# A selective-scan, attention and feed-forward kernel on one core: 32 channels by 4 states on the partitions, scans that end in PSUM, and a new set of due times

## The chip, the cores and the metric

One core of a Trainium2 chip runs the whole program in one launch. The metric is the device time of the launch in microseconds (us); smaller is better. Five engines work side by side: TensorE (PE) multiplies matrices into PSUM, VectorE (DVE) and ScalarE (ACT) work on SBUF and PSUM, GpSimd (POOL) works on SBUF, and SyncE (SP) issues the transfers here.

## The reference, cut to what matters

The input `x` has 8 images of 384 channels by 32x32 positions, 1024 tokens each. Per image the reference does this (all float32):

```
xn   = rmsnorm over channels of x
mamba(xn) forward, and backward over the reversed tokens:
    u, z  = split(in_proj(xn));   u = silu(causal conv over 4 tokens of u)
    dt, Bm, Cm = split(x_proj(u));  delta = softplus(dt_proj(dt))
    h[c, n, t] = exp(delta[c, t] * A[c, n]) * h[c, n, t-1] + delta[c, t] * u[c, t] * Bm[n, t]
    y[c, t]    = sum over 16 states n of h[c, n, t] * Cm[n, t]  + u * D
    result     = out_proj(y * silu(z))
y1   = x + res_scale * (scale_mod * (fwd + bwd) + sigmoid(3x3 depthwise conv of xn) * xn)
y2   = y1 + causal attention(layernorm(y1)) with rotary q and k
out  = feed-forward with gelu of layernorm(y2), plus y2
```

The recurrence over `t` for each of 384 channels and 16 states, in two directions, is the bulk of the elementwise work: 384 x 16 x 1024 x 2 values per image.

## The kernel before, in words

**Order.** Nothing in this kernel is issued where it is written. The class `Plan` records each instruction with a due time, measured in "units" of the scan (`plan.due`), and a `rush`; then `Plan.order` goes through a list schedule with its own cost for each kind of instruction, hands out the buffers named by `plan.tile(pool, shape, tag, bufs)`, and writes one fixed order for each engine. So all recorded instructions have the same line in the profile (the call in `issue`), and they are told apart by their tiles. Every engine works through its own list strictly in that order, and the lists depend on the constants at the head of the file: `SCAN`, `OTHERS`, `LAYER1` and so on are due times, and the numbers in `Plan` are costs. `_fill` adds matmuls of zeros (`y<-zero,ident`) where the planner sees TensorE idle; they add nothing to the sum in `y` and only keep TensorE busy.

**The scan.** An image has four steps (two directions by two halves of 512 tokens, `HB = 512`). A step is cut into 12 units (`n_u = NU * SG`). In a unit, the 128 partitions hold `CG` = 16 channels by `NE` = 8 states, and the free dimension holds `NQ` = 4 further channels of 512 tokens each, 2048 elements in all. A group of 64 channels takes `SG` = 2 units, one for each half of the 16 states. The tiles of a unit:

- `dl` (delta) and `du` (delta times u) are loaded from HBM (`dd`, `db`), each channel's row repeated on its 8 partitions: four transfers of 128x512 for each, once per group. `du` lies in a buffer of the tag `hs`, of which there are 5; `dl` has 5 buffers of 512.
- `br` and `cr` hold B and C, repeated over the channels: two loads of each per step. ACT copies `cr` into two PSUM banks, `cb`.
- POOL forms `hs = du * br` over 2048 elements.
- ACT forms `da = exp(dl * A)` four times, 512 elements each, in PSUM; the tag `da` has 3 banks.
- DVE runs `tensor_tensor_scan` four times, from `da` and `hs` into `hs`.
- In the steps where a half is followed by the next one, ACT copies the last column of `hs` to `carry`.
- `hs = hs * C` over 2048 elements, on DVE with `cb`, or on POOL with `cr` for the units in `POOL_C` (4 of 12) or `POOL_END`.
- PE sums over the states: four matmuls with the 0/1 matrix `sel` add the four quarters of `hs` to 32 rows each of the one PSUM bank `y`. Only then is the `hs` buffer free.

After the last unit of a 128-channel block, `y` leaves PSUM, either through ACT to `yd` in HBM or through DVE, times silu(z), to `side`.

**The rest**, spread between the units by `plan.spread`: `norm_in` (rmsnorm and the first half of in_proj; `xn` holds both halves of an image), `conv_tokens`, `prepare` (x_proj, dt_proj, softplus; writes `dd`, `db`, `bd`), `local_branch` (`gate`: the other half of in_proj; `conv`: the 3x3; `local`), then `project`, `attention` and `feed_forward` of the tokens that are done. Matmuls of these take one of two PSUM banks `w`; eight banks in all: 2 `w`, 3 `da`, 2 `cb`, 1 `y`. ACT has to load another table for silu, gelu or softplus and then again for exp.

Of the kernel before, what the change touches and what calls it, by code (L numbers as in the profile page):

```python
# [27 lines left out]
ALU = mybir.AluOpType  # L28
# [9 lines left out]
RUSH = 3.54  # L38
# [4 lines left out]
FIRST = (1.62, 3.88, 10.08, 14.37, 18.13, 22.35)  # L43
SECOND = (23.0, 0.55)
OTHERS = (4.41, 9.05, 14.9, 16.09, 22.99, 26.51, 31.92, 33.87, 42.68, 49.8)
BURST = 8.0
PROJECT = 1.86
LAYER1 = (39.24, 51.32, 61.95, 72.21, 83.3)
LAYER1_6 = (40.54, 50, 58.1, 65.96, 73.04)
LAYER1_7 = (39.38, 43.03, 45.9, 58.42, 62.69, 67.55, 71.01, 75.01, 81.01)  # L50
HASTE = 22.72
FREE = ["w", "da", "cb", "w", "da", "cb", "da"]
EXPS = 0.0
SCAN = (-1.59, -1.1, -0.46, -0.4, -0.36, 0.15, 0.79, 1.19)
class _Op:
# [4 lines left out]
        "busy", "early", "succ", "left", "ready", "preds", "issued",  # L60
# [16 lines left out]
class Plan:  # L77
# [8 lines left out]
    SWITCH = 1.3  # L86
    LOOSE = ("w", "tmp", "side")
    HURRY = 7.31
    PATIENCE = 1.81
    SETTLE = 0.2  # L90
    HOP = 0.18
    RATE = 300e3
    LAND = 2.54
    GATE = 3.413
    WARM, COLD = 0.8, 0.45
    KEEP = 0.65
    AHEAD = 9.0
# [41 lines left out]
    def add(self, eng, call, method, args, kw):  # L139
# [8 lines left out]
        op.tail, op.bytes = self.HOP, 0  # L148
        op.table, op.batch = None, self.batch
        if method == "dma_start":  # L150
            op.bytes = math.prod(outs[0].shape) * 4
            op.cost = 0.45 if eng == "sync" else 1.0
        elif eng == "tensor":
            once = kw.get("is_transpose") or method == "transpose"

            m = outs[0].shape[0]
            rate = 1.05 if once else 0.62 if m <= 32 else 1.0 if m <= 64 else 1.72
            op.cost = 0.02 + rate * max(n, 96) / 1e3
            op.busy = 0.75 if once else min(1.0, ins[0].shape[0] / 96)
            op.tail += self.SETTLE  # L160
        elif eng == "vector":
            scan = method == "tensor_tensor_scan"
            op.cost = 0.14 + (2.09 if scan else 1.04) * n / 1e3
            if method == "scalar_tensor_tensor":
                op.cost += 0.06
            if method in ("tensor_copy", "bn_aggr"):
                op.cost = 0.16
        elif eng == "scalar":
            aps = sum(1 for k, v in kw.items() if k in ("scale", "bias") and isinstance(v, bass.AP))
            op.cost = 0.21 + 0.714 * n / 1e3 + 0.05 * (method == "activation") + 0.06 * aps + 0.2 * ("accum_out" in kw)  # L170
            op.table = self.SETS.get(args[2]) if method == "activation" else self.set
        elif eng == "gpsimd":
            op.cost = (0.45 + 1.0 * n / 1e3) if len(ins) == 1 else (0.1 + 2.165 * n / 1e3)
# [93 lines left out]
    def _fill(self, t, now, begun):  # L267
# [5 lines left out]
        while work < self.KEEP * self.GATE:  # L273
# [3 lines left out]
            op.cost, op.busy, op.bytes, op.table = 0.02 + 1.72 * n / 1e3, 1.0, 0, None  # L277
# [8 lines left out]
    def order(self):  # L286
# [14 lines left out]
        drained = 0.0  # L301
# [53 lines left out]
        while issued < total:  # L355
# [36 lines left out]
            if op.bytes:  # L392
                drained = max(drained, end + 0.3) + op.bytes / self.RATE
                done = drained + self.LAND
                clock[e] = max(end, drained - self.AHEAD)
# [11 lines left out]
            for o in op.succ:  # L407
                o.left -= 1
                o.ready = max(o.ready, end if o.eng == e and not op.bytes else done)
# [17 lines left out]
def conv_attn_kernel(  # L427
# [31 lines left out]
    CG = 16  # L459
    NE = P // CG  # L460
    SG = NS // NE
    NQ = 4
    NU = C // (NQ * CG)
# [14 lines left out]
    def bank():  # L478
        rota.append(rota.pop(0))
        if rota[-1] == "w":  # L480
            return plan.tile(ps_w, [P, HB], "w", 2)
        return plan.tile(ps_b, [P, HB], rota[-1])
# [36 lines left out]
    dtw = weight([P, 2, C], "dtw")  # L519
    plan.vector.memset(dtw, 0.0)  # L520
    for d in range(2):
        plan.sync.dma_start(dtw[d * HP : d * HP + R, d], dt_wT)
# [42 lines left out]
    for to, at, n in ((up, 0, UP), (up, L + UP, UP), (xq, 0, WP + 1), (xq, XP - WP, WP)):  # L565
# [8 lines left out]
        logs.rearrange("c (j s) -> c j s", s=NQ * NS),  # L574
        a_log.rearrange("(j c q) n -> c j (q n)", c=CG, q=NQ),
# [25 lines left out]
    turn = "p (r q) -> p q r"  # L601
    for cc in range(NC):
        plan.gpsimd.tensor_scalar(
            ddiag[:, cc].rearrange("p (q r) -> p q r", q=NQ), ident.rearrange(turn, q=NQ),
            v_d[:, cc : cc + 1], None, ALU.mult,
        )

    held = weight([P, CG], "held")
    plan.vector.reduce_sum(held, ident.rearrange("p (c n) -> p c n", n=NE), axis=AX.X)
    sel = weight([P, 2, 2 * CG], "sel")  # L610
    plan.vector.memset(sel, 0.0)
    for i in range(2):
        plan.vector.tensor_copy(sel[:, i, i * CG : (i + 1) * CG], held)
# [34 lines left out]

    raw = plan.tile(l0, [P, NQ, HB], "hs", 5).rearrange("p q t -> p (q t)")[:, : NC * C]
    raw = raw.rearrange("p (cc e) -> p cc e", cc=NC)  # L650
    plan.sync.dma_start(raw, in_wT[:, C:].rearrange("(cc p) e -> p cc e", p=P))
    wz = weight([P, NC, C], "wz")
    for cc in range(NC):
        for m in range(NC):
            cols = slice(m * P, (m + 1) * P)
            plan.gpsimd.tensor_copy(
                wz[:, cc, cols].rearrange("p (q r) -> p q r", q=NQ),
                raw[:, cc, cols].rearrange(turn, q=NQ),
            )
    wout = weight([P, NC, C], "wout")  # L660
    for cc in range(NC):
        plan.sync.dma_start(
            wout[:, cc], out_wT[cc * P : (cc + 1) * P].rearrange("(r q) e -> q r e", q=NQ)
        )
# [47 lines left out]
    xn_t, z_t = {}, {}  # L712
# [11 lines left out]
    def xn_of(b, h):  # L724

        return xn_t[b][:, :, h * HR : (h + 1) * HR, :W]

    def norm_in(b, h):
        xt = load_x(b, h)
        yield  # L730
        if b not in xn_t:
            xn_t[b] = plan.tile(l0, [P, NC, H, WP], "xn")
        xn = xn_of(b, h)
# [13 lines left out]
        padded = xn_t[b][:, :, h * HR : (h + 1) * HR]  # L747
# [8 lines left out]
        for m in range(NC):  # L756
# [10 lines left out]
            yield  # L767

# [31 lines left out]
    def local(b, h):  # L800
# [6 lines left out]
        for cc in range(NC):  # L807
            xt = tmp()
            plan.sync.dma_start(xt, xv[b, :, cc, cols])
            sgi = sg[:, cc].rearrange("p (r w) -> p r w", w=W)  # L810
            plan.gpsimd.tensor_mul(sgi, sgi, xn_of(b, h)[:, cc])
# [4 lines left out]
    def gate(b, h):  # L816

        z = z_t[b, h] = plan.tile(l0, [P, NC, HB], "uc", 2)
        for m in range(NC):
            pz = bank()  # L820
            for cc in range(NC):
                plan.tensor.matmul(
                    pz.rearrange("p (r w) -> p r w", w=W),
                    wz[:, cc, m * P : (m + 1) * P], xn_of(b, h)[:, cc],
                    start=cc == 0, stop=cc == NC - 1,
                )
            plan.scalar.copy(z[:, m], pz)
            yield
# [47 lines left out]
    def prepare(b, steps):  # L876
# [17 lines left out]
        for i, si in enumerate(steps):  # L894
# [3 lines left out]
                [plan.tile(dram, [NC * 2 * CG, NQ * HB], nm, 8) for nm in ("dd", "db")]  # L898
# [4 lines left out]
        def rates(i, cc):  # L903
            pd = bank()
            rows = len(steps) * HP
            plan.tensor.matmul(
                pd, dtw[:rows, i, cc * P : (cc + 1) * P], xd[:rows], start=True, stop=True
# [3 lines left out]
        def store(i, cc, pd):  # L911
# [6 lines left out]
            for kd, t in zip(kept[i], (dl, du)):  # L918

                rows = kd[cc * 2 * CG : (cc + 1) * 2 * CG]  # L920
                plan.sync.dma_start(rows.rearrange("r (q t) -> (r q) t", q=NQ), t)
# [26 lines left out]
    def scan(b, si, lo=0, hi=HB):  # L948
# [9 lines left out]
        br = []  # L958
        for g in range(SG):
            plan.due = t0 + g - 4.0  # L960
            br.append(plan.tile(l0, [P, HB], "br", 2)[:, :n])
# [3 lines left out]
        plan.due = t0 - 1.5  # L965
        cr = plan.tile(l0, [P, SG, HB], "cr")[:, :, :n]
        cb = []
        for g in range(SG):
            plan.due = t0 - 1.5 + 0.2 * g
            plan.sync.dma_start(  # L970
                cr[:, g], bd[NS + g :: SG, lo:hi].unsqueeze(0).to_broadcast([CG, NE, n])
            )
            plan.due = t0 + f * (g - 0.3)
            cb.append(plan.tile(ps_b, [P, HB], "cb", SG)[:, :n])
            plan.scalar.copy(cb[g], cr[:, g])

# [3 lines left out]
        def hold():  # L980
            if not pair:
                t = plan.tile(l0, [P, NQ * HB], "hs", 5)
                for o in range(0, NQ * HB, NQ * n)[:SG] if n < HB else (0,):
# [3 lines left out]
        for k in range(n_u):  # L987
            q, g = divmod(k, SG)
            cc, part = divmod(q, 2)
            t = t0 + f * k  # L990
            if g == 0:
                rows = slice(q * CG, (q + 1) * CG)
                plan.due = t - 3.6
                du = hold()

                begin = b == 0 and si == 0 and k == 0
                for i in range(NQ):
                    plan.sync.dma_start(
                        du[:, i],
                        db[rows, i * HB + lo : i * HB + hi].unsqueeze(1).to_broadcast([CG, NE, n]),  # L1000
                    )
                plan.due = t - 3.4
                dl = []
                for i in range(NQ):
                    if i * n % HB == 0:
                        both = plan.tile(l0, [P, HB], "dl", 5)
                    dl.append(both[:, i * n % HB : i * n % HB + n])
                    plan.sync.dma_start(
                        dl[-1],
                        dd[rows, i * HB + lo : i * HB + hi].unsqueeze(1).to_broadcast([CG, NE, n]),  # L1010
                    )
                if part == 0:
                    plan.due = t - 2.0
                    parts = []
                    if ud is not None:
                        parts.append((ddiag[:, cc], ud[cc * P : (cc + 1) * P, lo:hi]))
                    if si >= 2:
                        parts.append((ident, y_t[b, h, cc][:, lo:hi]))
# [455 lines left out]
```

## Time and profile before

| what | value |
|---|---|
| time, three runs | 3198.13 us median (3196.02 to 3198.74) |
| the profiled execution: span | 3199.6 us, granted TensorE clock 0.964 |
| PE busy | 2770.0 us (87%), of which the matmuls of zeros 349.7 us |
| POOL busy | 2693.5 us (84%) |
| DVE busy | 2675.7 us (84%) |
| ACT busy | 2189.8 us (68%), 160 table loads of 1283 ns among it |
| DMA | 762.47 MB, 78.5% of 16 engines' span on SP's queue |

The span is that of the profiled execution, which is the one whose durations are used below; it lies 1.5 us over the median, within a thousandth. "Busy" is the time with at least one instruction of the engine running; a busy PE can still be waiting in part, since matmuls are pipelined and their ends modelled. In the lists of waits, a row "A x <- B y: us, times, longest" says how long engine A stood idle ahead of an instruction that writes tile x until engine B's instruction that writes y ended. "L423" stands in all of them.

### The profile page before, as it was taken

The page shows a single profiled execution, that of the slowest core. Times are in us where ns is not written, and L with a number is a line of the kernel's source. Part 1 is how long each engine was busy: PE and PEld are TensorE (multiplying, and loading weights), DVE is VectorE, ACT ScalarE, POOL GpSimd, SP SyncE. Part 2 cuts the span into 40 slices and gives each one's busy share as a digit, 9 for nine tenths or more (in the row PEclk, how much of TensorE's full clock was granted, in tenths as well). Part 3 has the DMA queues.
Part 4 walks back from the last instruction along what each step waited for, and adds up shares of the span by engine and source line. Part 5 has one row for each costly group of instructions (what it writes and reads, how often), then busy time and mean ns, then how long its engine had stood idle before and what let it go on. Part 6 is the DMA issues. An engine that isn't in the chain of part 4 may idle for free. (4 is left out here: it accounts for less than half of the span.)

```text
span 3199.6 us, 39939 instructions
## 1 busy us (share of the span) xinstructions
PE 2770.0 (87%) x11855; PEld 1160.9 (36%) x11855; DVE 2675.7 (84%) x2740; ACT 2189.8 (68%) x3591; POOL 2693.5 (84%) x923
## 2 busy tenths in 40 slices
PE   7887888888988989899888888898898998787789
PEld 3323333343333334343333433334343433343345
DVE  3778778897898889997899978988799979998972
ACT  3566676867677776868578676767768686666564
POOL 2888887788998889889889888888898989998950
PEclk9998999999999999999999998999999999999899
DMA  7998997878979887887978788798878879665530
GB/s 232 289 293 259 285 286 224 260 230 260 265 229 279 250 248 242 270 251 239 266 239 268 237 252 249 223 279 243 262 236 258 259 237 279 196 197 175 174 100 12
DMA packets 424462, 762.47 MB, mean 238 GB/s; under 512 B 51020, under 2 KB 70804, under 8 KB 424244
## 3 DMA queue, kind: packets, MB, share of 16 engines
q1 hardware_dynamic: 424116, 759.80, 78.5%
q8 instruction: 93, 1.52, 0.2%
q14 instruction: 125, 1.02, 0.1%
q0 software_dynamic: 128, 0.11, 0.0%
HBM read 617.92 MB, written 141.80 MB: 237 GB/s over the span
## 5 line engine op out<-in xcount | busy, mean ns | idle before, releaser
L423 POOL TENSOR_TENSOR hs<-hs,br 128x2048 f32<-128x2048 f32 (+1 forms) x395 | 1737.6, 4406 | 312.6 <-PE y L423 156.1
L423 ACT ACTIVATE da<-dl,nega 128x512 f32<-128x512 f32 (+1 forms) x1584 | 1056.6, 677 | 534.5 <-DVE hs L423 384.0
L423 DVE TENSOR_TENSOR_SCAN hs<-da,carry,hs 128x512 f32<-128x512 f32 (+1 forms) x816 | 935.7, 1201 | 125.1 <-ACT da L423 113.7
L423 DVE TENSOR_TENSOR_SCAN hs<-da,hs 128x512 f32<-128x512 f32 x768 | 883.9, 1202 | 132.6 <-ACT da L423 115.5
L423 POOL TENSOR_TENSOR hs<-hs,cr 128x2048 f32<-128x2048 f32 (+1 forms) x137 | 599.0, 4372 | 30.1 <-DVE hs L423 23.3
L423 DVE TENSOR_TENSOR hs<-hs,cb 128x2048 f32<-128x2048 f32 (+1 forms) x259 | 574.1, 2217 | 44.4 <-ACT carry L423 38.4
L423 PE MATMUL y<-hs,sel 128*32 128x512 f32 (+1 forms) x3168 | 446.7, 607 | 91.2 <-POOL hs L423 54.5
L423 PE MATMUL y<-zero,ident 128*128 128x256 f32 x1304 | 349.7, 398 | 0.0
L423 PEld LDWEIGHTS y<-zero,ident 128*128 128x128 f32 x1304 | 237.9, 195 | 144.7 <-issue 121.4
L423 PE MATMUL w<-rep,cit 96*32 96x512 f32 x1152 | 199.2, 657 | 34.1 <-DMA rep<-xq 26.3
L421 ACT ACT_TABLE_LOAD x160 | 205.3, 1283 | 2.8
L423 PE MATMUL w<-v,p 128*128 128x384 f32 x546 | 196.5, 506 | 10.4 <-ACT p L423 9.3
L423 PEld LDWEIGHTS y<-hs,sel 128*32 128x32 f32 x3168 | 80.9, 110 | 339.3 <-DVE hs L423 128.6
L423 PE MATMUL w<-q,fc1s 128*128 128x512 f32 (+1 forms) x388 | 191.0, 607 | 12.8 <-ACT p L423 6.0
L423 PE MATMUL w<-rep,cwt 128*32 128x512 f32 x744 | 162.1, 613 | 28.8 <-DMA rep<-up 13.6
L423 PE MATMUL w<-wout,side 128*128 128x384 f32 x378 | 146.4, 515 | 31.7 <-DVE side L423 22.3
L423 ACT ACTIVATE uc<-w,vec 128x512 f32<-128x512 f32 x144 | 97.1, 680 | 109.4 <-PE w L423 91.4
L423 ACT COPY gl<-w 128x512 f32<-128x512 f32 (+2 forms) x254 | 136.7, 549 | 23.4 <-PE w L423 21.2
L423 PE MATMUL w<-xn,wz 128*128 128x512 f32 x288 | 135.5, 614 | 11.3 <-ACT uc L423 5.0
L423 PEld LDWEIGHTS w<-v,p 128*128 128x128 f32 x546 | 101.4, 194 | 100.3 <-ACT p L423 31.2
L423 PE MATMUL w<-xn,win 128*128 128x512 f32 x288 | 133.5, 605 | 4.6 <-ACT tmp L423 4.4
L423 PE MATMUL w<-wvs,gl 128*128 128x384 f32 x372 | 135.4, 502 | 0.8 <-ACT uc L423 0.6
(204 smaller groups left out, 3191.8 us busy)
## 6 DMA issues: line engine op xcount, KB each, us to landing
dl<-dd SPq DMA_DIRECT2D x744, 256.0 KB, 5.4
hs<-db SPq DMA_DIRECT2D x744, 256.0 KB, 5.6
rep<-up SPq DMA_DIRECT2D x180, 257.5 KB, 6.4
rep<-xq SPq DMA_DIRECT2D x192, 222.4 KB, 7.1
tmp<-in_x_dram SPq DMA_DIRECT2D x96, 256.0 KB, 5.4
dd<-tmp SPq DMA_DIRECT2D x96, 256.0 KB, 3.7
db<-uc SPq DMA_DIRECT2D x96, 256.0 KB, 4.2
br<-bd SPq DMA_DIRECT2D x62, 256.0 KB, 5.8
```

The source lines that it names most:

```text
L421: self.nc.scalar.preload_act_table_set(table)
L423: op.call(*args, **{k: self._bind(v) for k, v in op.kw.items()})
```

## The change

Four things change together.

1. **Layout.** `CG` = 32 channels by `NE` = 4 states lie on the partitions, so `SG` = 4 units share one group of 128 channels, and there are three groups in a step, not six. `dl` and `du` are loaded three times per step; `br` and `cr` are four loads each. `sel` has one form; `wz`, `wout` and `ddiag` need no permuted columns. The number of units, exponentials and scans stays.
2. **Scan in PSUM.** In units whose multiply by C is on DVE (`split`), each scan writes over its exponential `da`, the carry is copied from there, one column for each scan, and DVE multiplies `hs[:, i] = da * cr[g]` 512 elements at a time. `cb` is gone, and `da` has 5 banks. The four matmuls of such a unit have due times of their own. Units with the multiply on POOL stay as they were.
3. **Input by halves.** `xn` holds one half. The gate's matmuls run right after `norm_in` (`raw_gate`), their result goes to HBM (`zr`) and comes back in `gate`; `local` loads `xn` from `xq`.
4. **Costs and due times** of the planner are other numbers: matmuls, ScalarE, transfers (with eight lanes for SP), and all constants of the schedule.

```diff
-SCAN = (-1.59, -1.1, -0.46, -0.4, -0.36, 0.15, 0.79, 1.19)
+SCAN = (-1.68, -1.03, -0.46, -0.42, -0.39, 0.15, 0.05, 1.19, 0.92)
+DU_AHEAD = 3.6
+DL_AHEAD = 4.52
+DLS = 5
+DAS = 5
...
-            rate = 1.05 if once else 0.62 if m <= 32 else 1.0 if m <= 64 else 1.72
-            op.cost = 0.02 + rate * max(n, 96) / 1e3
+            rate = 0.85 if once else 0.43 if m <= 32 else 0.84 if m <= 64 else 1.676
+            op.cost = rate * max(n, 64) / 1e3
...
-    CG = 16
+    CG = 32
...
-    NQ = 4
-    NU = C // (NQ * CG)
+    NQ = P // CG
+    NU = NC
...
+    def raw_gate(b, h):
+
+        xn, z = xn_t[b, h], plan.tile(dram, [P, NC, HB], "zr", 4)
+        zr_t[b, h] = z
+        for m in range(NC):
+            pz = bank()
+            for cc in range(NC):
+                plan.tensor.matmul(
+                    pz.rearrange("p (r w) -> p r w", w=W),
+                    wz[:, cc, m * P : (m + 1) * P], xn[:, cc],
+                    start=cc == 0, stop=cc == NC - 1,
+                )
+            zt = tmp()
+            plan.scalar.copy(zt, pz)
+            plan.sync.dma_start(z[:, m], zt)
+            yield
...
+            xn = reps()[:, : HR * WP]
+            at = 1 + (h * HR + 1) * WP
+            plan.sync.dma_start(xn, xq[cc * P : (cc + 1) * P, at : at + HR * WP])
...
-            cb.append(plan.tile(ps_b, [P, HB], "cb", SG)[:, :n])
-            plan.scalar.copy(cb[g], cr[:, g])
...
+            split = k not in (POOL_END if b == NB - 1 else POOL_C)
...
-                da = plan.tile(ps_b, [P, HB], "da", 3)[:, :n]
+                da = plan.tile(ps_b, [P, HB], "da", DAS)[:, :n]
...
-                o, a = hs[:, i], da
+                o, a, r = hs[:, i], da, da if split else hs[:, i]
...
-                plan.vector.tensor_tensor_scan(o, a, o, init, ALU.mult, ALU.add)
...
+                plan.vector.tensor_tensor_scan(r, a, o, init, ALU.mult, ALU.add)
+                if split:
+                    if save:
+                        plan.due, plan.rush = t + f * SCAN[5] * (i + 0.1), RUSH
+                        plan.scalar.copy(carry[:, k, i : i + 1], da[:, 0:1] if d else da[:, n - 1 :])
+                        plan.rush = 0.0
+                    plan.due = t + f * (SCAN[5] * i + SCAN[6])
+                    plan.vector.tensor_mul(hs[:, i], da, cr[g])
...
-                plan.vector.tensor_mul(hs, hs, cb[g].unsqueeze(1).to_broadcast([P, NQ, n]))
...
             for i in range(NQ):
+                plan.due, plan.rush = t + f * (SCAN[7] - 0.2 * (NQ - 1 - i) * split), RUSH
                 plan.tensor.matmul(
-                    y[i * 2 * CG : (i + 1) * 2 * CG], sel[:, part], hs[:, i],
-                    start=False, stop=done, skip_group_check=True,
+                    y[i * CG : (i + 1) * CG], sel, hs[:, i],
+                    start=g == 0 and not parts, stop=done, skip_group_check=True,
```

The program as built differs in these counts (before, after): matmuls of zeros 652, 916; DVE multiplies by C 259 (245 of 2048 elements, 14 of 1024), 1036 (980 of 512, 56 of 256); scans 1584, 1584, of which 1036 now write `da`; ACT copies to `carry` 204, 603; ACT copies to `cb` 66, none; table loads 161, 157; POOL's multiplies unchanged, its nine copies to `wz` gone; SP's transfers 2998, 2448.

## The prediction

> **What bounds it now.** I read the engines' shares first, then windows, then the waits of the engines that carry the scan, then a stretch of timeline that shows one of those waits.
>
> ```profile
> PE 2770.0 (87%) x11855; PEld 1160.9 (36%) x11855; DVE 2675.7 (84%) x2740; ACT 2189.8 (68%) x3591; POOL 2693.5 (84%) x923
> ...
> 800.00:2800.00 2000.00, 1759.90 (x7622) 723.08 (x7626) 1781.36 (x1767) 1436.78 (x2328) 1793.85 (x594) 0.97 0.83 250
> ```
>
> In the 2000 us in the middle (second row; columns PE, PEld, DVE, ACT, POOL busy), DVE is at 89% and POOL at 90%. No engine is full; two are nearly so and each waits for the other. The first 160 us (POOL busy 88) and the last 100 (POOL 10) are start and tail, and little in them changes. What can be won is the idle time in between. Waits of DVE, POOL and ACT (us, times, longest):
>
> ```profile
> DVE hs L423 <- ACT da L423: 229.2, 91, 6.8
> DVE hs L423 <- ACT carry L423: 38.6, 22, 5.2
> ...
> POOL hs L423 <- PE y L423: 156.1, 49, 10.5
> POOL hs L423 <- DMA hs<-db: 70.8, 15, 31.4
> ...
> ACT da L423 <- DVE hs L423: 384.0, 485, 5.2
> ACT da L423 <- DMA dl<-dd: 117.7, 87, 5.0
> ```
>
> DVE is idle 3199.6 - 2675.7 = 524 us; its largest wait is for exponentials. POOL is idle 506 us; its largest wait is for PE to free an `hs` buffer. Yet ACT itself waits 384 us for a free `da` bank: it could run ahead and has nowhere to write. The timeline of ACT and DVE shows how that hurts:
>
> ```profile
> 1498.43 1.28 ACT L421 ACT_TABLE_LOAD   x1
> 1499.72 2.77 ACT L423 ACTIVATE gl<-gl 128x3072 f32<-128x3072 f32 x1
> 1502.39 0.57 ACT L423 COPY uc<-w 128x512 f32<-128x512 f32 x1
> 1502.98 1.28 ACT L421 ACT_TABLE_LOAD   x1
> 1504.28 0.69 ACT L423 ACTIVATE da<-dl,nega 128x512 f32<-128x512 f32 x1
> ...
> 1505.00 1.22 DVE L423 TENSOR_TENSOR_SCAN hs<-da,hs 128x512 f32<-128x512 f32 x1 [5.42 <-ACT da L423]
> 1506.14 0.66 DVE L423 TENSOR_TENSOR p<-w,p 128x512 f32<-128x512 f32 x1
> 1506.72 1.21 DVE L423 TENSOR_TENSOR_SCAN hs<-da,hs 128x512 f32<-128x512 f32 x1
> 1507.85 2.26 DVE L423 TENSOR_TENSOR hs<-hs,cb 128x2048 f32<-128x2048 f32 x1
> 1510.03 7.90 DVE L423 TENSOR_TENSOR_SCAN hs<-da,hs 128x512 f32<-128x512 f32 x7
> ```
>
> ACT leaves exp for one gelu: 1498.43 to 1504.28, 5.9 us. DVE ran dry for 5.42 of it. There are 160 table loads, so about 80 such detours; 229 / 80 = 2.9 us of DVE each.
>
> [...]
>
> **The change, part by part.**
>
> *DVE multiplies.* Next start minus start in the timeline: 512 elements 1506.72 - 1506.14 = 0.58; 2048 elements 1510.03 - 1507.85 = 2.18. Four quarters cost 4 x 0.58 - 2.18 = +0.14, by 245 = 34 us, and about 2 for the 14 halves: **+36 of DVE**, all on an engine that binds.
>
> *Scans into PSUM.* Before has no scan that writes PSUM. [...] so I take 0[...].
>
> *Five banks for three.* Per scan DVE works 1.14 + 2.18/4 = 1.7 us. Three banks, one under the scan, leave two ready: 3.4 us of cover. Five, each held through its multiply, leave four: 6.8 us. That is up to 3.4 us more per detour, enough for most of the 2.9; but ACT must have filled the banks, and it also makes PE's evacuations. I take 229 to 90: **-140**. What is late next is POOL's product.
>
> *Carry.* The multiply no longer overwrites what the copy reads: 38.6 to about 9, **-30**. ACT pays: 399 more copies x 0.195 = +78, `cb` gone = -38 (62 x 0.59 and 4 halves): +40, under its 384 us of bank waits; 72% of the new span. Without that cover it would add 40.
>
> *hs buffers.* Before, per two units, a `du` is held from its load 3.6 units ahead to the last matmul, about 7 units, and one other for 3: 10/2 = all 5 buffers. After, per four units: `du` about 8, three others 3 each: 17/4 = 4.25. Release also comes sooner: after a unit's last scan there is a 0.58 multiply and not 2.18. POOL's 156 us behind `y` I take to 60, **-96**; part of it were DVE's stalls handed on.
>
> *Transfers.* `dl`, `du`: 744 fewer of 262 KB and 48 fewer of 131 KB, -201 MB. `br`, `cr`: +34. `zr` out and in +25, `xn` back in +13. Net 762 to about 633 MB, DMA share 79% to about 65%. POOL's waits for `db` without the first one of 31.4 us are 39: halved, **-20**. ACT's 117.7 for `dl` halve too, within its slack. SP issues 550 fewer at some 0.5 us; its lane frees 290 us. New: `gate` and `local` wait for loads of 5 us issued early; `tmp` (5 buffers) is held longer by `zr` stores. Off the path at 65% DMA; else some 5 us on each of 16 halves, +80.
>
> *PE.* The gate's matmuls only move; they and their copies are the same count. Two things add. Fills: +264 x 0.43 us (in the timeline of the start three in a row took 1.57 us and two 1.14) = +114. And `sel` matmuls: four to different 32-row groups run together in
>
> ```profile
> 1510.19 1.07 PE L423 MATMUL y<-hs,sel 128*32 128x512 f32 x8
> 1511.18 1.13 PE L423 MATMUL w<-p,emat 128*128 128x512 f32 x2
> 1512.14 0.60 PE L423 MATMUL w<-ident,t 128*128 128x128 f32 x4
> ```
>
> 0.99 us (1510.19 to 1511.18), as long as one lone 512-column matmul (1511.18 to 1512.14). In the built order of before these come in about 420 such groups, after in about 615, many of one or two. +195 x 0.85 (0.43 x 2 for 512 columns) = +165, less where a 32-row neighbour overlaps: +150. So PE gains about **265 us** of work. By pace rather than by busy time, 0.43 per 256 columns over the built order, PE goes from about 2410 to 2670, 75% to 86% of the span. Most lies in PE's gaps; I let a tenth reach the path, **+25**.
>
> *POOL.* Nine `wz` copies (0.4 each) go; they lay in the start, ahead of its 31.4 us wait: 0.
>
> *Due times.* They rearrange everything above; no row prices them: 0, and +-40 by the size of a 1% shift.
>
> **Sum** on the profiled 3199.6 (the median is 1.5 lower). DVE: +36 - 140 - 30 = 3066. POOL: -96 - 20 = 3084. The later engine sets the end, plus PE's 25: 3109, less 1.5, about **3110**, own range 3070 to 3150.
>
> **Rivals.**
> - *More* (0.12): POOL's buffer waits go with DVE's stalls altogether and PE's extra hides: near DVE's 3066[...]. For it: all waits above are each other's echoes. Against: POOL at 90% would have to reach 94%.
> - *The wait moves* (0.14): table loads and the carry copies in ACT's queue keep DVE waiting, so only 30 + 20 + some 20 of the rest come less 36: about 3165. For it: in-order ACT puts evacuations among the exponentials. It touches "no change" at its edge.
> - *Slower, PE binds* (0.16): split `sel` groups and 264 more fills stand ahead of the matmuls that free `hs` and `w`. 2670 of pace at 82.5% is 3237, so about 3240. The point is 2670/3198 = 83.5%: if PE can't be kept above that, the change loses. For it: 86% is above anything before shows over the whole span (75%), and POOL already waits for `y`. Against: PE in before mostly waits for others ("PE y <- POOL hs", "DVE hs").
> - *It doesn't do what it says*: the built order has the 1036 quarter multiplies, mostly one or two instructions behind their scans, and half the `dl` loads. Set aside.
>
> **Numbers.** Forecast case 0.58. A change under 0.2% (6 us) can't be told from none. Faster: 0.58 + 0.12 + 0.09 of the third case = 0.79; same 0.04; slower 0.17. Range 3035 to 3205: it leaves out the lowest edge of "more" and most of the slower case, under 0.2.
>
> **What would show it.** Right: "DVE hs <- ACT da" near 90 us though the tile is now `da`; carry waits under 15; POOL behind `y` near 60; DMA about 633 MB; DVE busy near 2712 and POOL's 2690. Wrong: scans of `da` far from 1.20 us; PE busy up and POOL or ACT waiting longer for PE than before; POOL idle still above 450 us.

## The result, and the profile after

The changed kernel takes 3193.05 us (median; before it, in the same series, 3196.06). The ratio is 0.9983, with a 95% interval of 0.9972 to 0.9994: a gain of 0.17%, under the 0.2% set as the least that can be told. The forecast was 3110. The profiled execution has a span of 3191.0 us and a granted clock of 0.982 (before 0.964).

First the engines' shares and the middle 2000 us (columns of the second row: stretch, length, busy time of PE, PEld, DVE, ACT, POOL, then PE's clock, DMA share, GB/s):

```profile
PE 2982.2 (93%) x12383; PEld 1270.4 (40%) x12383; DVE 2707.4 (85%) x3514; ACT 2166.1 (68%) x3920; POOL 2688.0 (84%) x914
...
DMA packets 345838, 632.80 MB, mean 198 GB/s; under 512 B 42544, under 2 KB 57208, under 8 KB 345624
...
800.00:2800.00 2000.00, 1922.20 (x8054) 808.50 (x8053) 1805.26 (x2283) 1420.65 (x2545) 1786.45 (x595) 1.00 0.64 209
```

DVE and POOL stand where they stood, at 90% and 89% of the middle. PE has gone from 88% to 96% of it, at full clock. The transfers did shrink, to 64% of the engines' time.

The waits of DVE, POOL and ACT after the change:

```profile
DVE hs L437 <- ACT carry L437: 72.0, 76, 4.9
DVE hs L437 <- ACT da L437: 49.5, 15, 8.8
DVE sm L437 <- PE w L437: 43.5, 41, 3.4
DVE da L437 <- ACT da L437: 37.5, 20, 8.4
...
POOL hs L437 <- PE y L437: 109.1, 43, 5.3
POOL hs L437 <- ACT carry L437: 85.8, 31, 6.8
POOL hs L437 <- DMA cr<-bd: 72.5, 3, 64.0
...
ACT da L437 <- DVE hs L437: 294.5, 368, 4.3
ACT uc L437 <- PE w L437: 120.1, 66, 8.7
ACT tmp L437 <- PE w L437: 98.4, 100, 6.0
```

The wait for exponentials did fall, 229 us to 49.5 + 37.5 = 87. Waits for PE and for carry copies came in its place. Summed over all rows of an engine, ACT waits 473 us for PE (before 263) and DVE 178 (before 111).

Two of the three signs that the prediction named for being wrong are there: ACT waits longer for PE, and POOL is idle for 3191.0 - 2688.0 = 503 us.

The last piece is in PE's own timeline (start us, length, tile; one matmul of 512 columns is two records):

```profile
1572.71 1.04 PE L437 MATMUL y<-hs,sel 128*32 128x512 f32 x2
1573.69 2.01 PE L437 MATMUL y<-zero,ident 128*128 128x256 f32 x8
1575.62 1.29 PE L437 MATMUL y<-hs,sel 128*32 128x512 f32 x4
1576.84 2.44 PE L437 MATMUL y<-zero,ident 128*128 128x256 f32 x10
1579.22 1.04 PE L437 MATMUL y<-hs,sel 128*32 128x512 f32 x2
1580.19 1.14 PE L437 MATMUL y<-zero,ident 128*128 128x256 f32 x4
```

One unit's four state sums come as one, two and one, with zeros between. The pieces of one take 1573.69 - 1572.71 = 0.98 us and 0.97, the pair 1.22. Together that is 3.2 us of PE for what took 0.99 us in one group before. ("Group" stands for state sums that follow each other directly on PE.) Over the whole kernel this is the group of the state sums:

```profile
L437 PE MATMUL y<-hs,sel 128*32 128x512 f32 (+1 forms) x3168 | 658.5, 602 | 40.7 <-POOL hs L437 34.2
```

The same 3168 records took 446.7 us busy in the kernel before:

```profile
L423 PE MATMUL y<-hs,sel 128*32 128x512 f32 (+1 forms) x3168 | 446.7, 607 | 91.2 <-POOL hs L423 54.5 <-DVE hs L423 34.5 <-DVE sm L423 1.2
```

The matmuls themselves are no longer (602 ns, before 607); fewer of them overlap.

### The profile page after: what moved, and what is told of

Its sections match the earlier page's. It is cut to its first block, busy times and chain, and to the rows that moved or that the text cites. A ratio compares the mean times of both kernels' runs of the same rounds, so it can differ in the third digit from the quotient of the medians.

```text
span 3191.0 us, 40113 instructions
## 1 busy us (share of the span) xinstructions
PE 2982.2 (93%) x12383; PEld 1270.4 (40%) x12383; DVE 2707.4 (85%) x3514; ACT 2166.1 (68%) x3920; POOL 2688.0 (84%) x914
## 2 busy tenths in 40 slices
DMA packets 345838, 632.80 MB, mean 198 GB/s; under 512 B 42544, under 2 KB 57208, under 8 KB 345624
## 4 chain that ended last, share of the span: by engine, by line
PE 51%; DVE 11%; ACT 10%; issue 4%; POOL 4%; DMA 1%; SPq 0%; ACTq 0%; POOLq 0%; DVEq 0%
PE w L437 35%; PE y L437 15%; DVE hs L437 4%; DVE da L437 4%; POOL hs L437 3%; ACT gl L437 3%; ACT da L437 2%; ACT L435 2%; ACT p L437 1%; ACT uc L437 1%; POOL uc L437 1%; DVE sm L437 1%; PE da L437 1%; ACT tmp L437 1%; DVE side L437 0%
## 5 line engine op out<-in xcount | busy, mean ns | idle before, releaser
L437 DVE TENSOR_TENSOR hs<-da,cr 128x512 f32<-128x512 f32 (+1 forms) x1036 | 658.6, 663 | 74.7 <-ACT carry L437 72.0
L437 POOL TENSOR_TENSOR hs<-hs,cr 128x2048 f32<-128x2048 f32 (+1 forms) x137 | 599.8, 4378 | 120.3 <-ACT carry L437 85.8
L437 PE MATMUL y<-hs,sel 128*32 128x512 f32 (+1 forms) x3168 | 658.5, 602 | 40.7 <-POOL hs L437 34.2
L437 DVE TENSOR_TENSOR_SCAN da<-da,carry,hs 128x512 f32<-128x512 f32 (+1 forms) x532 | 628.2, 1217 | 33.1 <-ACT da L437 21.6
L437 DVE TENSOR_TENSOR_SCAN da<-da,hs 128x512 f32<-128x512 f32 x504 | 594.7, 1214 | 37.3 <-POOL hs L437 17.7
L437 PE MATMUL y<-zero,ident 128*128 128x256 f32 x1832 | 486.2, 397 | 0.0
L437 PEld LDWEIGHTS y<-zero,ident 128*128 128x128 f32 x1832 | 327.6, 192 | 225.2 <-issue 189.3
L437 DVE TENSOR_TENSOR_SCAN hs<-da,carry,hs 128x512 f32<-128x512 f32 (+1 forms) x284 | 325.8, 1188 | 21.9 <-ACT da L437 13.7
L437 DVE TENSOR_TENSOR_SCAN hs<-da,hs 128x512 f32<-128x512 f32 x264 | 305.9, 1202 | 42.5 <-ACT da L437 35.8
L437 PEld LDWEIGHTS y<-hs,sel 128*32 128x32 f32 x3168 | 124.2, 110 | 376.3 <-issue 191.3
L437 ACT COPY carry<-da 128x1 f32<-128x1 f32 x532 | 79.4, 162 | 121.1 <-DVE da L437 119.6
```

Source lines behind the costliest of these rows:

```text
L437: op.call(*args, **{k: self._bind(v) for k, v in op.kw.items()})
```

## The experiments

Two theories stood first. PE: the split state sums (and perhaps the zeros) filled TensorE, which took the gain back. ACT: the carry copies did, standing in ScalarE's list among evacuations. A third, ORDER, was that the lists leave 10% idle whatever any one engine does. Most kernels below edit only the finished lists in `issue`, so the planner's order stays as it is.

| kernel | time, us | ratio to the kernel before (95%) | groups of state sums |
|---|---|---|---|
| changed kernel | 3193.05 | 0.9983 (0.9972 to 0.9994) | 615 |
| state sums together | 3093.16 | 0.9668 (0.9639 to 0.9696) | 396 |
| no zeros | 3199.09 | 1.0002 (0.9988 to 1.0015) | 580 |
| together, no zeros | 3126.16 | 0.9769 (0.9740 to 0.9798) | 396 |
| carry after multiply | 3199.88 | 1.0010 (0.9996 to 1.0024) | 615 |
| together, carry after multiply | 3112.30 | 0.9727 (0.9703 to 0.9751) | 396 |
| together, three banks | 3259.39 | 1.0190 (1.0159 to 1.0221) | 396 |
| together, more traffic | 3177.32 | 0.9938 (0.9912 to 0.9964) | 396 |
| kernel before, sums split | 3264.70 | 1.0208 (1.0175 to 1.0241) | 580 (before: 422) |
| planner waits for all four | 3139.46 | 0.9812 (0.9783 to 0.9841) | 465 |
| planner waits, then together | 3112.01 | 0.9734 (0.9709 to 0.9760) | 396 |

A group is counted from the built order: state sums that follow each other on PE, at most four to a group. Without the zeros some pieces become neighbours, hence 580 and not 615.

**The state sums together.** Each unit's matmuls are tagged, and all four go to the place of the last:

```diff
-            for op in self.order():
+            ops = self.order()
+            last = {op.batch: i for i, op in enumerate(ops) if op.batch and op.batch[0] == "sel"}
+            moved = {}
+            for i, op in enumerate(ops):
+                moved.setdefault(last.get(op.batch, i), []).append(op)
+            ops = [op for i in sorted(moved) for op in moved[i]]
+            for op in ops:
...
+                plan.batch = ("sel", b, si, lo, k)
                 plan.tensor.matmul(
```

> The changed kernel with one edit: in TensorE's finished list the four state-sum matmuls of a unit are put together, at the place of the last of them; every other list stays. Theory PE (TensorE sets the pace: its chain share is 51% and it is busy 96% of the middle 2000 us): the state sums fall from 658 us busy to about 450 as before the change, the time falls by half of that or more, to 3090 or less. Theory ACT (the scan waits for ScalarE's carry copies, which stand behind its evacuations): the time stays within 0.5% of 3193. Theory ORDER (the lists themselves, POOL against DVE, leave 10% idle whatever TensorE does): within 0.5% too.

The time falls by 100 us to 3093, with nothing else moved; the expectation had 3090 or less. The page of this kernel, the same middle stretch and the state sums:

```profile
PE 2844.8 (92%) x12383; PEld 1249.5 (40%) x12383; DVE 2701.1 (87%) x3514; ACT 2165.4 (70%) x3920; POOL 2688.0 (87%) x914
...
800.00:2800.00 2000.00, 1876.63 (x8287) 820.82 (x8286) 1871.64 (x2368) 1475.94 (x2642) 1862.96 (x612) 0.99 0.65 212
...
L443 PE MATMUL y<-hs,sel 128*32 128x512 f32 (+1 forms) x3168 | 494.2, 600 | 45.5 <-POOL hs L443 33.5
```

DVE and POOL now work 94% and 93% of the middle. The sums fell by 164 us, not quite to before's 447. ACT's and DVE's waits for PE fell to 351 and 126 us, and POOL's for `y` to 83.8. Over all rows of waits, DVE waits 472 us before this edit and 382 after it, POOL 452 and 360: both engines got back about 90 us. Theories ACT and ORDER can't give this. One piece of the evidence in the expectation was weak, though: PE's 51% of the chain. The chain of before covers only its last part (18% of the span), and another run with nearly these lists (carry after multiply) has 4%. Those shares depend on how far back the chain could be followed.

**No zeros.** One line in `issue` leaves out every TensorE instruction that belongs to no planned tile:

```diff
+            ops = [op for op in ops if op.eng != "tensor" or op.tiles]
```

> The changed kernel with the 916 matmuls of zeros left out of TensorE's finished list; every other list stays. Theory PE: 486 us of TensorE's 2982 busy us go, the time falls to 3050 to 3120, if the granted clock stays near 0.98. If the clock falls clearly below 0.95, the fills pay for themselves and the time does not fall. Theory ACT and theory ORDER: within 0.5% of 3193.

> Both edits, state sums together and no matmuls of zeros. Theory PE: TensorE busy near 2300, no longer a bound, and the forecast's 3110 or less appears: 3020 to 3100. Theory ACT and theory ORDER: within 0.5% of 3193.

The theory missed half here. Without zeros, PE's busy time falls to 2672 us and the time does not: 3199, as the expectation had it for a lower clock. With the sums together PE is busy 2562 us, not 2300, and the time is 3126, worse than with the zeros (3093). The granted clocks are 0.924 and 0.919 against 0.98, and each matmul of the sums takes longer, 637 ns for 602:

```profile
L439 PE MATMUL y<-hs,sel 128*32 128x512 f32 (+1 forms) x3168 | 706.2, 637 | 165.5 <-POOL hs L439 99.9
```

So the matmuls of zeros cost nothing on balance even here. All 916 were taken out, so the runs don't show what the 264 added ones do alone, nor how much of the result is the lower clock. The split sums are where the gain went: putting them together is worth 100 us with the zeros and 73 without.

**The carry copy after the multiply.** Copy and multiply of one bank are tagged as a pair, and the copy is issued behind the multiply:

```diff
+                        plan.batch = ("carry", b, si, lo, k, i)
                         plan.scalar.copy(carry[:, k, i : i + 1], da[:, 0:1] if d else da[:, n - 1 :])
...
+            ops = [op for i in sorted(moved) for op in sorted(moved[i], key=lambda op: op.eng == "scalar")]
```

> The changed kernel with one edit: each carry copy from a bank is issued after DVE's multiply from that bank, not ahead of it; DVE's list stays, ScalarE's copies move a few places back. Theory ACT: DVE's 72 us of waits for carry go below 15 and the time falls by 50 us or more. Theory PE: the wait turns into another one, the time moves by less than 0.5%. Theory ORDER: the same, less than 0.5%.

> The state sums together (3093 us) and each carry copy issued after DVE's multiply from the same bank. Theory ACT-NEXT (with TensorE relieved, the carry copies are the next bound: DVE waits 50 us and POOL 55 us for them): the DVE wait goes, 3040 to 3070. Theory HANDED-ON (in ScalarE's list the copy then waits for the multiply, and the exponentials behind it with it): 3085 to 3110, and DVE waits for exponentials instead.

DVE's waits for the carry went, and the time did not fall: 3199.88 for 3193, and with the sums together 3112 for 3093, 19 us worse. The wait was handed on, as one theory said (it had 3085 to 3110). In the second kernel ACT's list shows it:

```profile
ACT carry L443 <- DVE hs L443: 287.8, 323, 6.5
ACT da L443 <- DVE hs L443: 215.5, 218, 4.1
```

ACT now stands 288 us ahead of its copies, and DVE's wait for exponentials rises from 78 to 112 us. The order that the change chose is the better one.

**Three banks.** What did the parts of the change that worked bring? First the banks:

```diff
-DAS = 5
+DAS = 3
...
-            return plan.tile(ps_w, [P, HB], "w", 8 - 1 - DAS)
+            return plan.tile(ps_w, [P, HB], "w", 2)
```

> The state sums together, but the tag of the exponentials has 3 PSUM banks and not 5 (2 banks stay unused, 2 for the other matmuls); the planner makes new lists for it, with 1010 matmuls of zeros. Theory BANKS (five banks give the gain that shows once TensorE is relieved): DVE's wait for exponentials goes from 78 us back above 200 and the time to 3180 or more. Theory TRANSFERS (the gain is the halved loads): below 3130.

3259 us, 166 more than with five banks. DVE's waits for exponentials:

```profile
DVE da L443 <- ACT da L443: 129.6, 63, 10.8
...
DVE hs L443 <- ACT da L443: 59.8, 32, 7.4
```

Together they are 189 us, a little under the 200 expected, and POOL waits 193 us for `y`. Two banks stay empty and the planner makes new lists, so part of the 166 may be the lists'. Nor is it the kernel before with its three banks: here most banks are held through a multiply as well.

**More traffic.** At issue, each load of `du` or `dl` is followed by one of the same source into a spare in HBM:

```diff
                 op.call(*args, **{k: self._bind(v) for k, v in op.kw.items()})
+                if op.batch == "twice":
+                    spare.append(spare.pop(0))
+                    op.call(spare[-1][:, : args[0].shape[-1]], args[1])
```

> The state sums together, and each load of du or dl is followed by a transfer of the same source to a spare buffer in HBM that nobody reads: some 200 MB more, DMA share back near 79% or above, SyncE's list longer by 792 transfers. Theory TRANSFERS: 3120 to 3200, with POOL and ACT waiting for db and dd as before the change. Theory BANKS: within 1% of 3093.

834 MB (before the change 762) and 3177 us: 84 us for 201 MB. POOL's waits for transfers, all rows summed, rise from 93 to 166 us. So the halved loads seem to carry part of the gain as well, against the expectation of theory BANKS. The 84 us are not their price alone, since each added transfer writes to HBM, where the loads of before wrote to SBUF, and SyncE's list is now longer than before the change (3240 transfers for 2998). Banks and transfers can't be added, as each was tried with the other in place.

**The kernel before, its sums split.** The converse: in 167 units of the kernel before, PE's next other matmul goes between the second and third sum.

```diff
+            for places in at.values():
+                p = places[2]
+                n = next((j for j in range(places[3] + 1, len(ops)) if ops[j].eng == "tensor"), None)
...
+                taken.add(n)
+                before[p] = n
```

> The kernel before with one edit: in TensorE's finished list, for 167 of the 396 units the next other matmul is put between the second and third of the four state sums, so that they stand in about 580 separate groups, not 422 (the changed kernel: 615). Theory PE-PRICE (a group of one or two costs as much as one of four, and the path pays where TensorE is near full): busy of the state sums from 447 to about 570 us, PE busy near 2890; TensorE was at 87%, so the time rises by 10 to 60 us. If splitting costs nothing by itself and only the changed kernel's order is at fault: within 0.3% of 3196 and the busy time of the sums unchanged.

It takes 3264.7 us, 66 more than the kernel before in the same series (3198.5), a little over the upper end. The sums and the longest wait of POOL in this kernel:

```profile
L444 PE MATMUL y<-hs,sel 128*32 128x512 f32 (+1 forms) x3168 | 606.4, 607 | 113.9 <-POOL hs L444 80.1
...
POOL hs L444 <- PE y L444: 245.9, 65, 13.1
```

Busy time rises from 446.7 to 606.4 us, and POOL's wait for `y` from 156 to 246. So splitting reaches the path in a kernel that has nothing else of the change, at 87% busy: PE need not be full for it. The edit also puts the third and fourth sums behind another matmul; how much of the 66 us is that later place, and how much PE's added time, the run doesn't tell.

**The cure in the planner.** Each state sum is recorded as reading the whole `hs` tile, and the four have one due time:

```diff
-                plan.due, plan.rush = t + f * (SCAN[7] - 0.2 * (NQ - 1 - i) * split), RUSH
+                plan.due, plan.rush = t + f * SCAN[7], RUSH
...
                     start=g == 0 and not parts, stop=done, skip_group_check=True,
                 )
+                plan.ops[-1].tiles.append((hs, False))
```

> The changed kernel with the cure put into the planner and not into the finished list: each state-sum matmul is recorded as reading the whole hs tile, so the planner lets the four start only when all four quarters are multiplied, and they have one due time. All lists are new; the sums stand in about 465 groups (changed kernel 615, sums put together by hand 396), 932 matmuls of zeros. Theory GROUPS (each group beyond 396 costs about 0.45 us of the time, by 100 us for 219 groups and 69 us for 158): 3093 + 69 x 0.45 = 3124, within 30 either way since the lists are new. Theory LIST (what helped was one lucky list): anywhere, 3190 as likely as 3100.

> As the one before, and the four then put together in TensorE's finished list: 396 groups. Theory GROUPS: within 1% of 3093, and below the kernel before it by 10 to 40 us. Theory LIST: no order between the two.

All lists are new in both, and both come out in the order of their groups: 3139 with 465, 3112 with 396. The new lists themselves cost some 19 us, as 3112 and 3093 have the same number of groups. Within a pair with otherwise equal lists the price of a group agrees: 100 / 219 = 0.46 us for the changed kernel, 73 / 184 = 0.40 without zeros, 66 / 158 = 0.42 for the kernel before, 27 / 69 = 0.40 here. No version beats the changed kernel with its sums put together by hand: 3093.

## Why the prediction was wrong, point by point

- **DVE's multiplies, +36:** DVE's busy time rose by 31.7 us, to 2707 (forecast 2712). Right.
- **Scans into PSUM, 0** (my assumption, as before has none): 1214 ns without and 1273 ns with a carry, against 1202 and 1263 for the scans to SBUF beside them. Some 11 ns each, 1036 x 0.011 = 11 us.
- **Five banks, -140:** the wait went from 229 to 87 us (forecast 90). The mechanism was right; with three banks of this kind it is 189 us again.
- **Carry, -30: wrong in kind.** I took the multiply to be free of the copy, as it no longer overwrites what the copy reads. But both read one PSUM bank, and in either order the later of the two is seen waiting for the earlier: DVE's multiply waits 72.0 us for the copy, and with the order turned round (and the sums together) ACT's copy waits 287.8 us for the multiply. Why one reader waits for the other is not shown. DVE's wait rose from 38.6 to 72.0 us, and POOL's behind carry copies from 6.2 to 98.6 (85.8 + 7.0 + 5.8). POOL's units with the copy from `hs` have not changed; that their copies come late because ACT waits for PE is argued, though the wait falls to 64 us with the sums together. The swap took away DVE's wait alone and put another in its place, so what the carry costs is not shown. ACT's busy time, taken to rise by 40 us, fell by 24.
- **`hs` buffers, 156 to 60:** measured 109, and 84 with the sums together. Overstated.
- **Transfers:** 632.80 MB (forecast 633). POOL's wait for `db` all but vanished (70.8 to 1.6), but the wait ahead of its first product, 31.4 us before, is now 64.0 us under the name `cr`, and that product starts at 77.9 us, 7 later than before. Over all transfers POOL's waits fell by 44 us, from 142 to 97 (forecast 20). ACT's for `dd` fell from 117.7 to 7.2.
- **PE, +25: the step that failed.** The count was right: about 615 groups for 420, and 916 for 652 matmuls of zeros. Of 265 us more pace I let a tenth reach the path, because PE seemed to have gaps. The profile shows 212 us more for the sums (forecast 150) and 137 more for the zeros (114), and putting the sums together gives back 100 us. The mis-sized term is the share on the path: of the 150 us for the sums I let 15 through, and it was near 100. (The sums together have 26 groups fewer than the kernel before; at 0.46 us each, the 193 groups that the change added make an estimated 89 us.) That PE mostly waits for others was my argument against this rival, and it did not carry: its 420 us of waits before are mostly for ACT (218), DVE (107) and POOL (55), which wait for it in turn (263, 111 and 157 us). The waits show the way that the delay takes: ACT waits for `w` 237 us before, 433 after and 320 with the sums together. Of the 90 us that DVE then gets back, 53 were waits for PE itself and 39 for ACT, mostly its carry copies and exponentials; of POOL's, 46 were for ACT and 27 for PE.

Without PE's 25 us the forecast's sum is 3083; with its sums together the kernel takes 3093. So the other steps hold as a sum to some 10 us, or some 20 if the 26 groups are counted. That is in part luck, for it doesn't hold in each term: carry and buffers gave less, the transfers more than I counted. The rival "slower, PE binds" had the mechanism, but half of its ground (the zeros) did not show in the runs, and its 3240 was too far. Why the planner splits the sums is shown in part: with one due time for the four and a wait for the whole `hs` tile it makes 465 groups and not 615. Which of the two does it was not tried, nor was the planner's price: 0.43 x 512 / 1000 = 0.22 us for a lone matmul of 32 rows, where one holds PE for 0.97.

## What to carry to other kernels

Matmuls of 32 output rows each were cheap here only side by side, since one alone held PE as long as four in a row (0.97 us and 0.99): count groups in the built order, not instructions, when a finer hand-off breaks them up. Ask which engine pays for an earlier start; here the earlier start of three matmuls freed nothing, since the buffer goes free only with the fourth. Nor is an engine at 87% busy sure to have slack: the kernel before paid 66 us of time for 160 us more in its state sums, its gaps being mostly waits for engines that wait for it in turn.

## What the runs showed of the hardware that I had not expected

- A single 512-column matmul with 32 output rows holds PE for 0.97 us (1579.22 to 1580.19 after the change), four of them for different rows in a row for 0.99 us (1510.19 to 1511.18 before it).
- The matmuls of zeros paid here: without them the granted clock fell from 0.98 to 0.92, and with the sums together the time rose by 33 us.
- A scan that ends in PSUM, over its own input, is only some 11 ns slower than one that ends in SBUF (1214 ns for 1202, 512 elements).
